# Segmented attention scores over 64 partitions, with a rotary exchange by ScalarE copies

## The chip, the cores and the metric

The program runs on one core of one Trainium2 chip. Its five engines each take instructions in an order fixed when the program is built: TensorE (PE; its weight loads are listed apart as PEld), VectorE (DVE), ScalarE (ACT), GpSimd (POOL) and SyncE (SP), which here issues nearly all DMAs. The metric is the device time of one execution in microseconds; lower is better. Everything on TensorE is fp32 here, and each fp32 product appears in the profile as two matmul instructions with two weight loads.

## The reference

A batch of 16 sequences of 256 tokens with 256 features goes through four residual steps:

```python
x = x + attn0(cross(x, side, embed))             # 16 heads of 16 features, rotary, causal
x = x + ffn0(cond(x, W[cat]))                    # fp4 quantize/dequantize, gate, up, down (704)
x = x + attn1(diffuse(x, zX, zY, zR))            # segmented attention: the change is here
x = x + moe(cond2(x, experts[idx]))              # 8 experts, top 2, one shared
```

The third step, cut to what matters:

```python
q, k, v = split(rmsnorm(seq) * g_norm @ W_qkv)           # 16 heads of 64 features
q = q * cos + rotate_half(q) * sin                       # pairs (even, odd) of features
k = k * cos + rotate_half(k) * sin
q, k, v = segments of 128 tokens                         # two segments a sequence
k = concat(pm[0], k); v = concat(pm[1], v)               # 16 persistent keys a head
p = softmax(where(mask, q @ k.T * 64**-0.5, -1e30))      # 128 x (16 + 128) a head and segment
out = (p @ v) @ W_out
```

## The kernel before

The program has two parts. The first, `woven` (line 292), holds the first three steps. Each is written as one or more generators that yield single operations; `weave` (line 182) is a planner that runs when the program is built. It keeps an estimated time at which each engine is free and each tile is written or read, takes from all generators the operation that can start soonest, and appends it to its engine's queue. Between operations with the same start the generator that stands earlier in the list wins. Costs come from `Unit.cost` (line 165): for a matmul the columns, divided by a factor `side` for small tiles (2 where at most 32 rows are used); for the others a fixed part and a part per element; a DMA costs SP 0.06 us and lands 4.5 us later. In `ready` an operation that overwrites a tile waits for the last write and read of what was there.

The generators in their order: `stage_a` and `stage_e` (first attention), three generators that quantize weights of the feed-forward, `stage_f` (feed-forward; when it ends, batch b may be diffused), `stage_p` (diffusion and projections), `stage_g` (scores and softmax), `stage_v` (values and output projection; at the fourth group of heads it stores x to a DRAM tile `xd`). `g.done` counts what is finished; with it `stage_p` may be three groups of four heads ahead of the values, `stage_g` two, and `stage_a` five batches ahead of the last store. There are 16 batches with four groups, 64 groups in all.

For each group, `project4` (line 897) loads weights (256 KB in two DMAs for q and k, then v and output weights), and computes q and k transposed: features on partitions. Feature pairs are split: tile half r = 0 holds the even features, r = 1 the odd ones, each with four heads of 32 features on 128 partitions. The rotary step is therefore a product with cos and one with sin over both halves (VectorE, tiles `f_t1` and `f_t2`), and a subtraction and an addition between halves (GpSimd, 256 elements each), into `f_q` for q and into `keys[n]` for k. `scores4` (line 955) computes the scores in two passes of two heads. A score of 64 features is two matmuls of 32 partitions, one for each half, added up in PSUM, with the two heads on different 32-partition strips of the array. VectorE then adds the mask and takes the maximum, ScalarE computes the exponentials with their sums, GpSimd multiplies by the reciprocal. `values4` transposes the probabilities and multiplies by the values and the output weights.

`stage_p` begins with what is loaded once: `lap`, cos and sin and their scaled copies, the product of persistent values with the output weights (`pmo`), and the persistent keys, copied into `keys[n]` by 16 GpSimd copies of 32x64.

`project_heads` (line 467) does the first attention's rotary step along the free axis, with a tile for each of the two products. `fetch_a` (line 413) loads a batch's `xT`, `fT`, `emb`, `f` and `x`.

The second part, `mixture` (line 1034), is ordered by the framework's own scheduler. It loads all 16 batches of x from `xd` into `xs`, then `b1`, `bs2`, the shared expert's weights `w1s` and `w2s`, then the weights of `conditioned` (line 1338), which projects 512 tokens at a time with a per-batch weight `own` loaded three deep, and routes the tokens; then shared blocks, expert tiles and combination follow.

Of the kernel before, what the change touches and what calls it, by code (L numbers as in the profile page):

```python
# [12 lines left out]
F32 = mybir.dt.float32  # L13
# [6 lines left out]
P = 128  # L20
# [42 lines left out]
def setup(ctx, tc, a, n_batch):  # L63
# [28 lines left out]
    k.zero = c.tile([P, D], F32, name="zero")  # L92
    nc.gpsimd.memset(k.zero, 0.0)

    k.xd = [dram.tile([S, D], F32, name=f"xd{b}") for b in range(n_batch)]
# [50 lines left out]
class Unit:  # L146
# [17 lines left out]
    def cost(self, fn, outs, ins):  # L164
        if self.name == "SP":
            return 0.06
        if self.name == "PE":
            if fn == "transpose":
                return 0.15
            lhsT, rhs = ins  # L170
            fp32 = 4 if rhs.dtype == F32 else 1
            rows, cols, n = lhsT.shape[0], row_size(lhsT), row_size(rhs)
            side = (2 if rows <= 32 else 1) * (3 if cols <= 32 else 2 if cols <= 64 else 1)
            return max((2 if fp32 == 4 else 1) * cols / 2070, fp32 * n / 2070 / side) + 0.01
        fixed, each = COSTS[self.name]
        n = max(row_size(x) for x in outs[:1] + ins)
        if fn == "reciprocal":
            each = 0.006
        return fixed + each * n + (0.3 if len(outs) > 1 else 0)


def weave(streams):
# [8 lines left out]
    def ready(op, engine):  # L191
# [4 lines left out]
        for x in op.outs:  # L196
# [7 lines left out]
            for p in before:  # L204
                if p:
                    t = max(t, p[0] + (HOP if p[1] != engine else 0.0))
# [85 lines left out]
def woven(k):  # L292
    nc, tc = k.nc, k.tc
    with ExitStack() as ctx:
# [12 lines left out]
        g.live, g.kT = {}, {}  # L307
        g.x, g.io, g.done = {}, {}, {"W": 0, "A": 0, "M": 0, "E": 0, "F": 0, "P": 0, "G": 0, "V": 0, "L": 0}
        with tc.manual_schedule():
            weave([stage_a(g), stage_e(g), stage_gate(g), stage_up(g), stage_down(g), stage_f(g), stage_p(g), stage_g(g), stage_v(g)])  # L310

# [101 lines left out]
def fetch_a(g, b):  # L413

    a = g.a
    g.x[b] = g.xp.tile([P, 2, D], F32, name="x", tag="x")
    xT = g.a_.tile([P, 2, S], F32, name="xT", tag="xT", bufs=2)
    fT = g.a_.tile([P, 2, S], F32, name="fT", tag="fT")
# [48 lines left out]
def project_heads(g, hT):  # L467
# [8 lines left out]
    for st in range(2):  # L476
# [11 lines left out]
        table = lambda t: t[:, st, :].unsqueeze(1).to_broadcast([P, 2 * H, DH0 // 2])  # L488
        t1, t2 = tile_a(g, 2 * D, "b_t1"), tile_a(g, 2 * D, "b_t2")
        for r in range(2):  # L490
            yield g.dve.tensor_tensor(pairs(t1)[:, :, :, r], pairs(qk)[:, :, :, r], table(g.cos0), ALU.mult)
            sin = table(g.sin0 if r else g.nsin0)
            yield g.dve.tensor_tensor(pairs(t2)[:, :, :, r], pairs(qk)[:, :, :, 1 - r], sin, ALU.mult)
        for i, dst in enumerate((qp, kp)):
            half = slice(i * D, (i + 1) * D)
            yield g.pool.tensor_tensor(dst[:, st, :, 0:DH0], by_head(t1[:, half]), by_head(t2[:, half]), ALU.add)

# [298 lines left out]


def stage_p(g):
    k, a = g.k, g.a
    yield lambda: g.done["A"] > 0 and g.done["W"] == 3  # L800
    g.lap, op = load(g, g.w, "lap", [P, 2, S], a["lap"])
# [36 lines left out]

    g.keys = []
    for n in range(4):  # L840
        pmk = tile_l(g, [P, 2, 4 * PM], "pmk", 2)
        yield g.sp.dma_start(out=pmk, in_=a["pmk"][:, n])
        t = g.w.tile([P, 2, 2, PM + P], F32, name=f"keys{n}")
        for j in range(4):
            rows = row32(j, 32)
            src = pmk[rows, :, j * PM : (j + 1) * PM]
            yield g.pool.tensor_copy(t[rows, :, :, 0:PM], src.unsqueeze(2).to_broadcast([32, 2, 2, PM]))
        g.keys.append(t)
    g.mhalf = g.w.tile([P, 2], F32, name="mhalf")
    yield g.pool.memset(g.mhalf, -0.5)  # L850
# [46 lines left out]
def project4(g, n, zT):  # L897

    a = g.a
    wq = tile_l(g, [P, 2, 2, 2 * P], "wq", 2)  # L900
    for which in range(2):
        cols = slice((8 * which + 2 * n) * P, (8 * which + 2 * n + 2) * P)
        yield g.sp.dma_start(out=wq[:, which], in_=a["w_qk1"][:, :, cols])
    wv, wo = tile_l(g, [P, 2, 4 * DH1], "wv", 2), tile_l(g, [P, 2, D], "wo", 3)
    yield g.sp.dma_start(out=wv, in_=a["w_v1"][:, :, n * 4 * DH1 : (n + 1) * 4 * DH1])
    yield g.sp.dma_start(out=wo, in_=a["w_out1"][:, 2 * n : 2 * n + 2, :])
    q = tile_l(g, [P, 2, S], "f_q", 3)
    by_seg = lambda t: t.rearrange("p (s t) -> p s t", s=2)
    for which in range(2):
        one = yield from single(g, wq, zT)  # L910
        pq = one.rearrange("p (r t) -> p r t", r=2)
        for r in range(2):
            yield from mm_(g, pq[:, r, :], [(wq[:, which, c, r * P : (r + 1) * P], zT[:, c, :]) for c in range(2)])
        t1, t2 = tile_l(g, [P, 2, S], "f_t1"), tile_l(g, [P, 2, S], "f_t2")
        cos, sin = (g.cos1, g.sin1) if which else (g.cosq, g.sinq)
        yield g.dve.tensor_tensor(t1, pq, cos.unsqueeze(1).to_broadcast([P, 2, S]), ALU.mult)
        yield g.dve.tensor_tensor(t2, pq, sin.unsqueeze(1).to_broadcast([P, 2, S]), ALU.mult)
        g.singles.append(one)
        dst = [g.keys[n][:, r, :, PM:] if which else by_seg(q[:, r, :]) for r in range(2)]
        yield g.pool.tensor_tensor(dst[0], by_seg(t1[:, 0, :]), by_seg(t2[:, 1, :]), ALU.subtract)  # L920
        yield g.pool.tensor_tensor(dst[1], by_seg(t1[:, 1, :]), by_seg(t2[:, 0, :]), ALU.add)
    v = tile_l(g, [P, 2, 4 * DH1], "f_v", 3)
# [4 lines left out]
    yield copy_(g, v, pv)  # L927
    g.singles.append(one)
    return q, v, wo

# [24 lines left out]
def scores4(g, n, q, v, wo):  # L955
# [8 lines left out]
    for j0 in (0, 2):  # L964
        two = yield from pair(g, q, keys)
        sc = [two[:, i, : 2 * (PM + P)].rearrange("p (s w) -> p s w", s=2) for i in range(2)]
        for st in range(2):
            for r in range(2):
                for i in range(2):
                    rows = row32(j0 + i, 32)  # L970
                    lhsT, rhs = q[rows, r, st * P : (st + 1) * P], keys[rows, r, st, :]
                    yield g.pe.matmul(sc[i][:, st, :], lhsT, rhs, start=r == 0, stop=r == 1)
        for i in range(2):
# [60 lines left out]
def mixture(k, out):  # L1034
# [5 lines left out]
    with ExitStack() as ctx:  # L1040
# [33 lines left out]
        for blk in range(early, NT // 4):  # L1074
# [5 lines left out]
            for t in range(4 * blk, 4 * blk + 4):  # L1080
                combine(k, r, t, out)


# [254 lines left out]
def conditioned(k, keep, r):  # L1338
# [3 lines left out]
    with ExitStack() as ctx:  # L1342
# [178 lines left out]
```

## Time and profile before

| What | Value |
|---|---|
| Median of 3 runs (lowest, highest) | 2903.49 us (2898.98, 2906.39) |
| Profiled execution | 2904.1 us |
| Its span | 2902.4 us |
| Mean granted TensorE clock | 0.964 |
| End of the woven part (last operation on x) | 1896.8 us |
| First conditioned matmul after it | 1926.8 us |
| DMA moved | 270.38 MB |

The span is the time from the first to the last recorded instruction. A group of instructions is listed by line, engine, operation and tiles (written <- read), its shape, its count, its busy time and mean in ns, and the idle time of its engine just before it with what ended that. Line 160 is the planner's helper, through which all operations of the woven part pass, so there the tiles tell which code an operation belongs to. [...]

The page's slices show the same in rough form: 40 equal slices of 72.6 us, a digit for tenths of busy time. The shared and expert blocks take the slices at the end.

```profile
PE 5899999999999999999999998869999999999999
DVE  6566666676676667766776665613332000000023
ACT  2223323333333333333333333313222222222221
POOL 4333333333334334433343333312331000000034
PEclk8799999999899999998999999979999999999999
```

### The profile page before, as it was taken

The page shows a single profiled execution, that of the slowest core. Times are in us where ns is not written, and L with a number is a line of the kernel's source. Part 1 is how long each engine was busy: PE and PEld are TensorE (multiplying, and loading weights), DVE is VectorE, ACT ScalarE, POOL GpSimd, SP SyncE. Part 2 cuts the span into 40 slices and gives each one's busy share as a digit, 9 for nine tenths or more (in the row PEclk, how much of TensorE's full clock was granted, in tenths as well). Part 3 has the DMA queues.
Part 4 walks back from the last instruction along what each step waited for, and adds up shares of the span by engine and source line. Part 5 has one row for each costly group of instructions (what it writes and reads, how often), then busy time and mean ns, then how long its engine had stood idle before and what let it go on. Part 6 is the DMA issues. An engine that isn't in the chain of part 4 may idle for free. (4 is left out here: it accounts for less than half of the span.)

```text
span 2902.4 us, 41871 instructions
## 1 busy us (share of the span) xinstructions
PE 2728.9 (94%) x15819; PEld 2056.7 (71%) x15819; DVE 1437.1 (50%) x3115; ACT 925.0 (32%) x2416; POOL 862.8 (30%) x1030
## 2 busy tenths in 40 slices
PE   5899999999999999999999998869999999999999
PEld 3666667777777777777677767735566788888866
DVE  6566666676676667766776665613332000000023
ACT  2223323333333333333333333313222222222221
POOL 4333333333334334433343333312331000000034
PEclk8799999999899999998999999979999999999999
DMA  3132122222131231231231122141112255555533
GB/s 109 55 95 74 53 90 70 65 93 70 59 99 59 67 101 45 74 108 35 79 104 44 62 88 66 52 144 46 49 48 84 76 190 191 191 193 201 192 100 106
DMA packets 196525, 270.38 MB, mean 93 GB/s; under 512 B 34912, under 2 KB 167264, under 8 KB 186976
## 3 DMA queue, kind: packets, MB, share of 16 engines
q1 hardware_dynamic: 190176, 250.87, 26.9%
q0 software_dynamic: 6144, 16.79, 1.9%
q8 instruction: 127, 2.08, 0.3%
q14 instruction: 78, 0.64, 0.1%
HBM read 207.05 MB, written 60.56 MB: 92 GB/s over the span
## 5 line engine op out<-in xcount | busy, mean ns | idle before, releaser
L160 ACT ACTIVATE f_prob<-pair,f_stat 128x144 f32<-128x144 f32 x512 | 191.1, 378 | 270.1 <-DVE f_stat L160 258.6
L160 DVE TENSOR_TENSOR pair<-pair,mask 128x256 f32<-128x256 f32 (+1 forms) x384 | 197.8, 515 | 123.1 <-PE pair L160 83.2
L160 PE MATMUL single<-e_zT,wq 128*128 128x256 f32 x1024 | 254.0, 392 | 0.0
L49 PE MATMUL bank<-ysT,w 128*128 128x256 f32 x1120 | 247.5, 379 | 0.2 <-ACT ysT L113 0.2
L1162 POOL DMA_INDIRECT got<-osort,pos_o x64 | 62.4, 974 | 623.5 <-PE bank L49 582.5
L49 PE MATMUL bank<-w,ehT 128*128 128x256 f32 x1120 | 247.5, 379 | 0.0
L1144 ACT ACTIVATE ehT<-bank,own_b 128x256 f32<-128x256 f32 x280 | 132.8, 474 | 348.8 <-PE bank L49 348.8
L49 PEld LDWEIGHTS bank<-ysT,w 128*128 128x128 f32 x1120 | 212.7, 190 | 29.4 <-ACT ysT L113 0.5
L49 PEld LDWEIGHTS bank<-w,ehT 128*128 128x128 f32 x1120 | 210.2, 190 | 27.2
L160 PEld LDWEIGHTS single<-e_zT,wq 128*128 128x128 f32 x1024 | 193.4, 196 | 32.8 <-issue 2.8
L160 POOL TENSOR_SCALAR_AFFINE_SELECT b_e<-b_e 128x512 f32<-128x512 f32 x128 | 86.8, 678 | 329.5 <-ACT b_e L160 329.5
L160 PE MATMUL pair<-keys,f_q 32*128 32x144 f32 x2048 | 164.9, 300 | 0.9 <-ACT b_e L160 0.7
L160 PEld LDWEIGHTS pair<-keys,f_q 32*128 32x128 f32 x2048 | 137.2, 190 | 35.9 <-issue 28.0
L160 ACT ACTIVATE b_e<-pair 128x768 f32<-128x768 f32 x128 | 103.7, 811 | 166.2 <-PE pair L160 153.5
L1152 DVE TENSOR_TENSOR eo<-bank,eb 128x512 f32<-128x512 f32 x35 | 24.2, 692 | 234.4 <-PE bank L49 234.4
L160 POOL TENSOR_TENSOR f_q<-f_t,f_t 128x256 f32<-128x256 f32 x128 | 91.8, 736 | 160.7 <-DVE f_t L160 151.3
L160 PE MATMUL single<-wo,f_oT 128*128 128x256 f32 x512 | 129.8, 386 | 9.5 <-ACT f_oT L160 8.4
L160 PE MATMUL pair<-b_qkT 16*128 16x128 f32 (+1 forms) x1024 | 126.9, 371 | 10.9 <-ACT b_qkT L160 7.9
L160 DVE TENSOR_REDUCE qpad<-pair 128x2 f32<-128x256 f32 (+1 forms) x256 | 131.0, 554 | 4.4
L160 DVE TENSOR_TENSOR x<-x,single 128x512 f32<-128x512 f32 (+1 forms) x112 | 68.0, 607 | 128.5 <-PE single L160 127.9
L160 POOL TENSOR_TENSOR keys<-f_t,f_t 128x256 f32<-128x256 f32 x128 | 95.3, 764 | 118.6 <-DVE f_t L160 117.5
L160 PE MATMUL pair<-b_qS,b_qkT 17*128 17x256 f32 (+1 forms) x1024 | 121.7, 357 | 6.2 <-DVE qpad L160 2.8
(290 smaller groups left out, 5235.7 us busy)
## 6 DMA issues: line engine op xcount, KB each, us to landing
w<-in_w SPq DMA_DIRECT2D x70, 1024.0 KB
ysort<-zero SPq DMA_DIRECT2D x32, 1024.0 KB
wq<-in_w_qk SPq DMA_DIRECT2D x128, 256.0 KB
wv<-in_w_v SPq DMA_DIRECT2D x64, 256.0 KB
wo<-in_w_out SPq DMA_DIRECT2D x64, 256.0 KB
ys<-ysort SPq DMA_DIRECT2D x35, 256.0 KB
osort<-eo SPq DMA_DIRECT2D x35, 256.0 KB
eb<-in_b SPq DMA_DIRECT2D x35, 128.0 KB
```

The source lines that it names most:

```text
L49: nc.tensor.matmul(out, lhsT, rhs, start=start and i == 0, stop=stop and i == last)
L160: return Op([(self.name, self.cost(fn, outs, aps), lambda: call(*args, **kw))], outs, aps)
L1144: nc.scalar.activation(hT[:, f, :], ph, AF.Gelu_apprx_tanh, bias=b1[:, f : f + 1])
L1152: nc.vector.tensor_tensor(o, po, b2.unsqueeze(1).to_broadcast([P, 2, D]), ALU.add)
L1162: nc.gpsimd.indirect_dma_start(out=g, out_offset=None, in_=k.osort[:, :], in_offset=bass.IndirectOffsetOnAxis(ap=r.pos_o[:, i, t : t + 1], ...
```

## The change

It has several parts.

- **Scores over 64 partitions.** A head's 64 features now lie together: even ones on 32 partitions, odd ones on the next 32. Two heads fill 128 partitions, and c counts two pairs of heads. A score is one matmul of 64 partitions, so `scores4` issues half as many.
- **Rotary exchange.** The partner of a feature is now on another strip of 32 partitions. After the sin product, ScalarE copies `t2` strip by strip into `t3` with neighbouring strips exchanged, four copies of 32 partitions by 512 elements for q and four for k; the sign is put into the sin tables once. GpSimd then adds once over 512 elements. That addition is yielded one step later (`join`). `f_t1` gets two buffers, `f_t3` has two, `f_t2` one.
- **Weights in the new order.** `stage_order` loads the q and k weights in eight steps, re-orders the columns with two GpSimd copies a step, and stores them to a DRAM tile `wqk`, from which `project4` then loads. The list of generators holds it twice, and each runs all eight steps. `stage_p` waits until the first has ended.
- **Persistent keys.** Eight small loads and four wider copies in place of four loads and sixteen copies.
- **Order.** `stage_g` stands before `stage_p`. The planner prices 33 to 64 rows with factor 1.5, and no longer holds an SP operation back for an earlier write or read by SP.
- **First attention.** The cosine product is done in place in `qk`, after the sine products; `xT` has one buffer.
- **Mixture.** Only batches 0 and 1 of x are loaded at the start, the others two ahead in `conditioned`; `w1s` and `w2s` are loaded after it.

```diff
@@ class Unit: cost; weave: ready
-            side = (2 if rows <= 32 else 1) * (3 if cols <= 32 else 2 if cols <= 64 else 1)
+            side = (2 if rows <= 32 else 1.5 if rows <= 64 else 1) * (3 if cols <= 32 else 2 if cols <= 64 else 1)
...
-                if p:
+                if p and not p[1] == engine == "SP":
                     t = max(t, p[0] + (HOP if p[1] != engine else 0.0))
@@ woven
-            weave([stage_a(g), stage_e(g), stage_gate(g), stage_up(g), stage_down(g), stage_f(g), stage_p(g), stage_g(g), stage_v(g)])
+            weave([stage_a(g), stage_e(g), stage_gate(g), stage_up(g), stage_down(g), stage_order(g), stage_order(g), stage_f(g), stage_g(g), stage_p(g), stage_v(g)])
@@ fetch_a
-    xT = g.a_.tile([P, 2, S], F32, name="xT", tag="xT", bufs=2)
+    xT = g.a_.tile([P, 2, S], F32, name="xT", tag="xT")
@@ project_heads
-        t1, t2 = tile_a(g, 2 * D, "b_t1"), tile_a(g, 2 * D, "b_t2")
+        t2 = tile_a(g, 2 * D, "b_t2")
         for r in range(2):
-            yield g.dve.tensor_tensor(pairs(t1)[:, :, :, r], pairs(qk)[:, :, :, r], table(g.cos0), ALU.mult)
             sin = table(g.sin0 if r else g.nsin0)
             yield g.dve.tensor_tensor(pairs(t2)[:, :, :, r], pairs(qk)[:, :, :, 1 - r], sin, ALU.mult)
+        for r in range(2):
+            yield g.dve.tensor_tensor(pairs(qk)[:, :, :, r], pairs(qk)[:, :, :, r], table(g.cos0), ALU.mult)
...
+def stage_order(g):
+
+    k = g.k
+    for i in range(8):
+        cols = slice(i * 2 * P, (i + 1) * 2 * P)
+        raw, out = tile_l(g, [P, 2, S], "f_t1", 2), tile_l(g, [P, 2, S], "f_t3", 2)
+        yield g.sp.dma_start(out=raw, in_=g.a["w_qk1"][:, :, cols])
+        for c in range(2):
+            dst = out[:, c].rearrange("p (j r d) -> p j r d", j=4, r=2)
+            yield g.pool.tensor_copy(dst, raw[:, c].rearrange("p (r j d) -> p j r d", r=2, j=4))
+        yield g.sp.dma_start(out=k.wqk[:, :, cols], in_=out)
+    g.done["O"] = 1
@@ stage_p
-    yield lambda: g.done["A"] > 0 and g.done["W"] == 3
+    yield lambda: g.done["A"] > 0 and g.done["W"] == 3 and g.done["O"]
...
+    for rows in (row32(1, 32), row32(3, 32)):
+        for t in (g.sin1, g.sinq):
+            yield g.pool.tensor_scalar(t[rows], t[rows], -1.0, None, ALU.mult)
@@ project4
-        yield g.sp.dma_start(out=wq[:, which], in_=a["w_qk1"][:, :, cols])
+        yield g.sp.dma_start(out=wq[:, which], in_=k.wqk[:, :, cols])
...
-        t1, t2 = tile_l(g, [P, 2, S], "f_t1"), tile_l(g, [P, 2, S], "f_t2")
+        t1, t2, t3 = (tile_l(g, [P, 2, S], f"f_t{i}", 1 if i == 2 else 2) for i in (1, 2, 3))
...
-        dst = [g.keys[n][:, r, :, PM:] if which else by_seg(q[:, r, :]) for r in range(2)]
-        yield g.pool.tensor_tensor(dst[0], by_seg(t1[:, 0, :]), by_seg(t2[:, 1, :]), ALU.subtract)
-        yield g.pool.tensor_tensor(dst[1], by_seg(t1[:, 1, :]), by_seg(t2[:, 0, :]), ALU.add)
+        for i in range(4):
+            yield g.act.copy(t3[row32(i, 32)], t2[row32(i ^ 1, 32)])
+        dst = g.keys[n][:, :, :, PM:] if which else q.rearrange("p c (s t) -> p c s t", s=2)
+        yield from join
+        join = iter([g.pool.tensor_tensor(dst, by_seg(t1), by_seg(t3), ALU.add)])
@@ scores4
-            for r in range(2):
-                for i in range(2):
-                    rows = row32(j0 + i, 32)
-                    lhsT, rhs = q[rows, r, st * P : (st + 1) * P], keys[rows, r, st, :]
-                    yield g.pe.matmul(sc[i][:, st, :], lhsT, rhs, start=r == 0, stop=r == 1)
+            for i in range(2):
+                rows, c = row32(2 * i, 64), j0 // 2
+                lhsT, rhs = q[rows, c, st * P : (st + 1) * P], keys[rows, c, st, :]
+                yield g.pe.matmul(sc[i][:, st, :], lhsT, rhs, start=True, stop=True)
@@ mixture, conditioned
-        for b in range(B):
-            nc.sync.dma_start(out=k.xs[:, 2 * b : 2 * b + 2, :], in_=k.xd[b].rearrange("(s p) d -> p s d", p=P))
+        for b in range(2):
+            load_x(k, b)
...
+        conditioned(k, keep, r)
         nc.sync.dma_start(out=w1s, in_=a["w1"][NE])
         nc.sync.dma_start(out=w2s, in_=a["w2"][NE])
-        conditioned(k, keep, r)
...
+                if b + 2 < B:
+                    load_x(k, b + 2)
```

More of the change, by code (lines that the diff above doesn't have):

```diff
@@ L93, in setup @@
     nc.gpsimd.memset(k.zero, 0.0)
+    k.wqk = dram.tile([P, 2, 2 * H * DH1], F32, name="wqk")
     k.xd = [dram.tile([S, D], F32, name=f"xd{b}") for b in range(n_batch)]
@@ L307, in woven @@
         g.live, g.kT = {}, {}
-        g.x, g.io, g.done = {}, {}, {"W": 0, "A": 0, "M": 0, "E": 0, "F": 0, "P": 0, "G": 0, "V": 0, "L": 0}
+        g.x, g.io, g.done = {}, {}, {"W": 0, "O": 0, "A": 0, "M": 0, "E": 0, "F": 0, "P": 0, "G": 0, "V": 0, "L": 0}
         with tc.manual_schedule():
-            weave([stage_a(g), stage_e(g), stage_gate(g), stage_up(g), stage_down(g), stage_f(g), stage_p(g), stage_g(g), stage_v(g)])
+            weave([stage_a(g), stage_e(g), stage_gate(g), stage_up(g), stage_down(g), stage_order(g), stage_order(g), stage_f(g), stage_g(g), stage_p(g), stage_v(g)])
 def load(g, pool, name, shape, src):
@@ L488, in project_heads @@
         table = lambda t: t[:, st, :].unsqueeze(1).to_broadcast([P, 2 * H, DH0 // 2])
-        t1, t2 = tile_a(g, 2 * D, "b_t1"), tile_a(g, 2 * D, "b_t2")
+        t2 = tile_a(g, 2 * D, "b_t2")
         for r in range(2):
-            yield g.dve.tensor_tensor(pairs(t1)[:, :, :, r], pairs(qk)[:, :, :, r], table(g.cos0), ALU.mult)
             sin = table(g.sin0 if r else g.nsin0)
             yield g.dve.tensor_tensor(pairs(t2)[:, :, :, r], pairs(qk)[:, :, :, 1 - r], sin, ALU.mult)
+        for r in range(2):
+            yield g.dve.tensor_tensor(pairs(qk)[:, :, :, r], pairs(qk)[:, :, :, r], table(g.cos0), ALU.mult)
         for i, dst in enumerate((qp, kp)):
             half = slice(i * D, (i + 1) * D)
-            yield g.pool.tensor_tensor(dst[:, st, :, 0:DH0], by_head(t1[:, half]), by_head(t2[:, half]), ALU.add)
+            yield g.pool.tensor_tensor(dst[:, st, :, 0:DH0], by_head(qk[:, half]), by_head(t2[:, half]), ALU.add)
 def row32(j, n):
@@ L839, in stage_p @@
     g.keys = []
+    pmk = tile_l(g, [P, 4, 2, PM], "pmk")
+    for j in range(4):
+        for r in range(2):
+            src = a["pmk"][row32(j, 32), :, r, j * PM : (j + 1) * PM]
+            yield g.sp.dma_start(out=pmk[row32(2 * (j % 2) + r, 32), :, j // 2, :], in_=src)
     for n in range(4):
-        pmk = tile_l(g, [P, 2, 4 * PM], "pmk", 2)
-        yield g.sp.dma_start(out=pmk, in_=a["pmk"][:, n])
         t = g.w.tile([P, 2, 2, PM + P], F32, name=f"keys{n}")
[L844 to L847, printed above, removed]
+        yield g.pool.tensor_copy(t[:, :, :, 0:PM], pmk[:, n].unsqueeze(2).to_broadcast([P, 2, 2, PM]))
         g.keys.append(t)
+    for rows in (row32(1, 32), row32(3, 32)):
+        for t in (g.sin1, g.sinq):
+            yield g.pool.tensor_scalar(t[rows], t[rows], -1.0, None, ALU.mult)
     g.mhalf = g.w.tile([P, 2], F32, name="mhalf")
@@ L897, in project4 @@
 def project4(g, n, zT):
-    a = g.a
+    k, a = g.k, g.a
     wq = tile_l(g, [P, 2, 2, 2 * P], "wq", 2)
@@ L907, in project4 @@
     q = tile_l(g, [P, 2, S], "f_q", 3)
-    by_seg = lambda t: t.rearrange("p (s t) -> p s t", s=2)
+    by_seg = lambda t: t.rearrange("p c (s t) -> p c s t", s=2)
+    join = ()
     for which in range(2):
@@ L928, in project4 @@
     g.singles.append(one)
+    yield from join
     return q, v, wo
@@ L1081, in mixture, with load_x @@
                 combine(k, r, t, out)
+def load_x(k, b):
+    k.nc.sync.dma_start(out=k.xs[:, 2 * b : 2 * b + 2, :], in_=k.xd[b].rearrange("(s p) d -> p s d", p=P))
 def shared_block(k, r, w1, w2, blk):
```

## The prediction

> **What bounds the kernel now.** I read the page first (busy shares, slices, chain), then the stretches by stage, then the groups by shape, then the order of time around the scores and around the hand-over to the mixture. The chain that ended last holds only the final shared block, so it says nothing on the place of the change.
>
> ```profile
> span 2902.4 us, 41871 instructions
> PE 2728.9 (94%) x15819; PEld 2056.7 (71%) x15819; DVE 1437.1 (50%) x3115; ACT 925.0 (32%) x2416; POOL 862.8 (30%) x1030
> ```
>
> TensorE is busy for 94% of the span, the next engine for half. An average over stages proves little, so next come the stretches: the woven stage with all streams, its tail (mostly segmented attention), the hand-over, the conditioned projection, and the start in two parts. Columns are start and end, length, busy time of PE, PEld, DVE, ACT and POOL, clock, DMA share, GB/s.
>
> ```profile
> 300.00:1700.00 1400.00, 1338.49 (x9191) 1011.11 (x9192) 959.91 (x1922) 508.57 (x1499) 533.66 (x635) 0.97 0.23 72
> 1700.00:1896.80 196.80, 172.89 (x1162) 139.44 (x1161) 108.08 (x213) 65.24 (x246) 67.30 (x81) 0.92 0.21 69
> 1896.80:1926.80 30.00, 4.20 (x18) 3.28 (x18) 1.83 (x8) 0.62 (x2) 3.47 (x15) 0.54 1.00 310
> 1926.80:2280.00 353.20, 350.46 (x1239) 212.21 (x1239) 104.53 (x402) 98.09 (x144) 79.98 (x72) 1.00 0.16 50
> ...
> 0.00:20.00 20.00, 0.22 (x1) 0.22 (x2) 1.23 (x3) 1.28 (x1) 6.78 (x16) 1.00 0.57 185
> 20.00:100.00 80.00, 65.23 (x331) 44.05 (x332) 55.14 (x117) 25.44 (x57) 34.74 (x44) 0.74 0.27 79
> ```
>
> From 300 to 1700 us TensorE idles 61.5 us of 1400 (4%); VectorE is at 69%, ScalarE at 36%. So TensorE sets the pace, and work taken from it there comes off the end, unless another engine starts to make it wait. In the tail it idles 24 of 197 us. In the hand-over it idles 26 of 30 us while the DMA engines are full (share 1.00, 310 GB/s). The groups that the change touches or copies:
>
> ```profile
> L160 PE MATMUL pair<-keys,f_q 32*128 32x144 f32 x2048 | 164.9, 300 | 0.9 <-ACT b_e L160 0.7 <-DVE vpad L160 0.2
> L160 POOL TENSOR_TENSOR keys<-f_t,f_t 128x256 f32<-128x256 f32 x128 | 95.3, 764 | 118.6 <-DVE f_t L160 117.5
> L160 POOL TENSOR_TENSOR f_q<-f_t,f_t 128x256 f32<-128x256 f32 x128 | 91.8, 736 | 160.7 <-DVE f_t L160 151.3 <-PE single L160 4.7 <-DVE f_stat L160 4.0
> L160 ACT COPY f_pT<-single 128x512 f32<-128x512 f32 x94 | 53.3, 587 | 55.5 <-PE single L160 53.3 <-DVE q_y L160 1.9
> ```
>
> Each fp32 product is recorded as two instructions: the code asks for 1024 score products, the profile shows 2048. In order of time, one pair of heads is 16 instructions:
>
> ```profile
> 1022.41 1.25 PE L160 MATMUL pair<-keys,f_q 32*128 32x144 f32 x16
> 1023.59 1.99 PE L160 MATMUL single<-wv,e_zT 128*128 128x256 f32 x8
> 1025.52 0.86 PE L160 MATMUL single<-b_e,vpad 128*32 128x256 f32 x16
> 1026.30 1.09 PE L160 MATMUL single<-f_pT,f_v 128*64 128x128 f32 x16
> 1027.33 0.44 PE L160 MATMUL single<-ident,b_oS 128*128 128x128 f32 x2
> ```
>
> From the start of the scores to the start of the next group: 1.18 us. The values (f_pT, f_v) are 16 instructions of 128 columns, two at a time: 1.03 us. Recorded ends overlap the next start, so starts are what to subtract.
>
> **What the Trainium skill says.** "TensorEngine Tiling (Array Packing)", section Tiling Modes: 64 rows by 128 columns is two tiles that run independently, 32 by 128 is four. "TensorE: Matmul & The Clock Gate", section Why this matters for your kernels: one matmul over 32 rows takes as long as one over 128; the gain is in running tiles at once. The trace agrees: eight full 128-row instructions of 256 columns (e_zT,wq at 1035.68, the next group at 1037.41) take 1.73 us, 0.85 ns a column, and sixteen score instructions of 144 columns at that rate would take 1.95 us one after another; they take 1.18, so they run two at a time. "ScalarE: Activation LUTs", section What ACT_TABLE_LOAD costs: an ACTIVATE with immediate operands takes 186 ns plus 0.833 ns an element, back-to-back ones overlapping by about 93 ns; for 512 elements 613 ns, the trace has 587. That ScalarE's queue is strictly first in, first out ("TensorE: Matmul & The Clock Gate", the table at its head) is what makes the added copies a risk.
>
> **Part by part.**
>
> Scores. Before, two heads run at once, each in two steps of 32 features; after, two heads at once, each in one step of 64. Of 16 instructions in a group 8 are left. Two at a time, a group takes half of 1.95, 0.97 us, plus 0.21 us of changing over to make 1.18; after, 0.48 + 0.21 = 0.69. The 0.2 is confirmed by the values: 16 x 128 x 0.85/2 ns = 0.87, measured 1.03. So 0.49 us less for each of 64 x 2 = 128 groups, 63 us at full clock. The page's mean group (164.9/128 = 1.29 against 1.25 us undisturbed) is 3% longer for the clock: 64 us. Bounds: the kernel's planner now prices 64 rows at 1.5 instead of 2 tiles' worth; if that is true, a group takes 0.64 + 0.21 = 0.85 and 42 us go; nothing supports more than 75 us (1.18/2 each).
>
> Rotary exchange. ScalarE gets 64 x 2 x 4 = 512 copies of 32 partitions by 512 elements. No row has 32 partitions from SBUF; the nearest is 587 ns (f_pT, from PSUM), the skill's price less overlap is 520. I take 587: 300 us more, 925 to 1225 us. In 300 to 1700 (46 of the 64 head groups) it is 46 x 4.7 = 216 us, so ScalarE goes from 36% to about 53%. GpSimd: 256 additions of 256 elements (187 us) become 128 of 512; at 1.28 us (a_qT's 1289 ns) 164 us, 23 us less. VectorE is unchanged. None of this is on TensorE. The path from projection to q or keys grows by 4 x 0.587 - 3 x 0.09 = 2.1 us and two hand-overs. Projections may be three head groups ahead of the values, about 3 x 27 us in the middle, so the latency is covered; without cover it would be 2.5 us x 64 = 160 us. What is not covered is the queue: behind four copies stand exponentials and PSUM evacuations that TensorE waits for (f_oT, f_pT, b_qkT: 17 of the 61.5 us idle), and on GpSimd, behind an addition waiting for its copies, stand b_e's masks and the quantization (d_h, c_y: 24 of the 61.5 us). The bounds are 0 (all planned around) and 100 us (one full block of copies, 2.1 us, at three out of four head groups). ScalarE's load grows by half, so I let the ScalarE and GpSimd part of the waits (50 us) grow by 30%: +15 us, tail included.
>
> Order. Scores get rank over projections. TensorE work is the same; in the tail it may shorten or lengthen the 24 us idle. I take 0 and leave +-10 in the range.
>
> The re-ordered weights. Two streams of eight steps each run the whole re-ordering twice: 16 loads and 16 stores of 256 KB, 8.4 MB, and 32 GpSimd copies of 128x256 (about 0.86 us, the cost of cosq's scaling of that shape: 27 us). At 310 GB/s the bytes are 27 us of DMA time; the first 100 us carry 100 GB/s, so they fit, but loads of weights queue behind them, and SP's queue stands while a store waits for its copy. Their SP instructions, 32 at about 0.45 us, are 14 us of a queue that waits most of the time. GpSimd goes from 42 to about 69 us in the first 100, and it carries the weight quantization, which gates the first feed-forward at about 101 us. TensorE idles 20 us at first anyhow. Bounds 0 and 40 us; I take +8.
>
> Hand-over. 14 of 16 loads of xs (8.7 of 9.9 us of SP's issue) and w1s and w2s (1.5 us) leave the front of SP's queue, with 3.7 + 2.1 = 5.8 MB. expb, issued at 1917.9 and the one that the first conditioned matmuls waited for (till 1924.6), is issued 10.2 us sooner, and 5.8 MB less at 310 GB/s is 18.7 us less queue. I take -12, bounds -5 and -19. The later loads come behind exp_w, a block (44 us) ahead of use, in a stage at 50 GB/s: hidden, and if not, 256 KB at 310 GB/s, 0.8 us each. w1s and w2s are needed about 2280 us, some 40 us after their new place.
>
> Edits with one answer: in-place cosine product (same four VectorE instructions; GpSimd still reads before the next is written), xT with one buffer (fT, loaded next, has one already), fewer but wider pm copies (4.3 us become about 5 with the sign changes, once), the planner's rule for SP after SP: 0, with SP's queue possibly standing some us at a time.
>
> **Sum**, against the profiled execution (2904.1 us, span 2902.4; the median of the runs is 2903.5, so no correction): -64 + 15 + 8 - 12 = -53, 2851 us.
>
> **Rivals.**
> A, as above: 2851, its own range 2815 to 2880. For it: 96% TensorE in the stage.
> B, 64-row tiles pack worse (1.5): -42 + 15 + 8 - 12 = -31, 2873. For it only the planner's constant; against it the values' rate.
> C, slower: ScalarE's queue takes the pace. Each of the 64 head groups adds two blocks of 2.1 us in front of exponentials; if 1.7 us of the 4.2 end up as TensorE idle, 64 x 1.7 = 109 us, and 2904 - 64 + 109 + 8 - 12 = 2945; with 1.2 us 2913. It decides from about 1.1 us a head group, where it has eaten 68 us. For it: exponentials already make GpSimd and VectorE wait, and in the tail a head group takes 12 us, of which copies would take 4.7 of ScalarE. Against it: ScalarE is half empty, and the planner prices copies about right.
> D, the start: the doubled re-ordering delays the first feed-forward by its full 40 us: 2883. For it, SP and GpSimd both in order; against it, its streams rank below those that load the weights.
>
> **How the numbers follow.** A 0.53, B 0.11, C 0.25 (2910 to 2960), D 0.11. A difference under 0.3% (9 us, 2895 to 2912) can't be told from none. Faster: A, B and D, with a tail of D and A taken off, 0.68; within: 0.08; slower: C, 0.24. The range goes from 2815 to 2925, which takes in A, B, D and the lower half of C. A alone has 2815 to 2880.
>
> **What would show it.** Scores as 64x144 x1024 with about 85 to 90 us busy and 0.69 us from start to start (B: 0.85). ScalarE 300 us more. TensorE idle in the woven stage up by no more than 25 us, waits for ScalarE or GpSimd grown by 15 (C: 80 and more). First conditioned matmul 10 to 15 us after the last store of x. First projection e_zT,wq at 187 us before, under 200 after (D: 220 and more). I am wrong if the stage's idle time grows by as much as its busy time shrinks.

## The result, and the profile after

The changed kernel takes 2981.57 us (median of four runs, 2972.64 to 2988.36), the kernel before beside it 2904.94 us: a ratio of 1.0264, 95% interval 1.0231 to 1.0297. It is 77 us slower; the forecast was 53 us faster. The profiled execution took 2988.4 us, 84 us more than that of before.

The page of the changed kernel: its first lines, then four engines and the granted clock in 40 slices of 74.7 us.

```profile
span 2986.6 us, 40424 instructions
PE 2735.1 (92%) x14795; PEld 2030.8 (68%) x14795; DVE 1478.6 (50%) x3157; ACT 1221.1 (41%) x2886; POOL 852.3 (29%) x926
PE   5899999979989999999889997769999999999999
DVE  6456667565777766676667775533343000000013
ACT  2234455445545455444545465533232232222221
POOL 5323233333433423333333332322332000000035
PEclk7779999899999999999999998879999999999999
```

TensorE has 1024 instructions fewer, and yet it is busy 6 us longer (2735.1 against 2728.9). Before, 9s ran almost unbroken through the woven part; now 7s and 8s stand in slices 9 and 12, in the middle (20 and 21) and in three slices at its end (25 to 27).

The stretches of the changed kernel (start and end, length, busy time of PE, PEld, DVE, ACT and POOL, clock, DMA share, GB/s): the same 1400 us as before, the rest of the woven part, the hand-over, the conditioned projection, and last the woven part from its first projection (`e_zT,wq`) to its end. Below it the same last stretch of the kernel before.

```profile
300.00:1700.00 1400.00, 1288.17 (x8120) 948.38 (x8122) 957.06 (x1888) 702.48 (x1767) 491.24 (x518) 0.95 0.21 68
1700.00:1996.80 296.80, 240.43 (x1370) 185.28 (x1368) 161.05 (x310) 160.11 (x443) 96.86 (x88) 0.91 0.21 68
1996.80:2011.00 14.20, 2.22 (x11) 1.87 (x11) 1.10 (x6) 0.64 (x2) 1.13 (x14) 0.56 0.80 224
2011.00:2360.00 349.00, 345.85 (x1225) 208.58 (x1225) 105.94 (x401) 98.17 (x144) 81.27 (x73) 1.00 0.22 68
205.80:1996.80 1791.00, 1614.46 (x10001) 1195.32 (x9999) 1182.24 (x2329) 905.73 (x2305) 622.97 (x643) 0.94 0.21 68
```

```profile
187.10:1896.90 1709.80, 1616.02 (x11025) 1226.51 (x11024) 1145.13 (x2289) 610.09 (x1833) 646.52 (x771) 0.97 0.23 71
```

The account of the 84 us closes with these. The first projection comes 18.7 us later (205.8 against 187.1). From there to the end of the woven part it takes 1791.0 us in place of 1709.8, 81.2 more. The hand-over is 15.7 us shorter (14.2 against 29.9). After it nothing differs. So the loss lies in the woven part, and there TensorE's idle time went from 93.8 us to 176.5, while its busy time stayed (1616.0, 1614.5) although a thousand instructions left it.

Why did it stay? The groups that the change touches, and one that it doesn't, by shape, after:

```profile
L161 PE MATMUL pair<-keys,f_q 64*128 64x144 f32 x1024 | 104.1, 318 | 9.9 <-POOL keys L161 9.0 <-ACT b_e L161 0.5 <-ACT f_prob L161 0.3
L161 PE MATMUL single<-e_zT,wq 128*128 128x256 f32 x1024 | 274.2, 415 | 41.2 <-DMA wq<-wqk 38.8 <-ACT e_zT L161 2.4
L161 ACT COPY f_t<-f_t 32x512 f32<-32x512 f32 x512 | 316.0, 617 | 146.4 <-DVE f_t L161 137.9 <-POOL f_q L161 0.6 <-DVE f_stat L161 0.4
L161 POOL TENSOR_TENSOR keys<-f_t,f_t 128x512 f32<-128x512 f32 x64 | 83.9, 1311 | 64.5 <-ACT f_t L161 63.6
```

The second of them before:

```profile
L160 PE MATMUL single<-e_zT,wq 128*128 128x256 f32 x1024 | 254.0, 392 | 0.0
```

The scores gave up 60.8 us (164.9 to 104.1). But 1024 instructions that nobody touched now take 415 ns each in place of 392, while the mean granted clock of the stretch fell from 0.97 to 0.94. (The granted clock is the share of its full clock that TensorE was given. The median instruction of this group takes 379 ns, the longest 792; in the trace the granted clock of a moment is either 1 or 0.5.) Summed over the stretch, the untouched instructions took back 59 us (-1.6 + 60.8). And a new wait stands in front of this group: 38.8 us for the DMA of `wq`, of which before had none. The lists of waits suggest where it comes from. Two of TensorE's and two of SP's longest waits after:

```profile
PE single L161 <- POOL f_prob L161: 39.1, 17, 6.4
PE single L161 <- DMA wq<-wqk: 38.8, 9, 6.1
...
SPq L161 <- PE single L161: 1011.2, 93, 57.1
SPq L161 <- DVE x L161: 345.8, 13, 53.7
```

Columns are total, times and longest, in us. SP waits 346 us for VectorE's last write of x, that is, at the store of x; before it did so for 67.1 us.

All of TensorE's waits in this stretch, summed by what they were for, account for nearly all of its idle time: GpSimd 56.1 us before and 71.2 after, ScalarE 25.0 and 27.8, VectorE 10.5 and 36.2, DMA 0 and 38.8. So of the 83 us more, only 18 are waits that ended with ScalarE or GpSimd; the rest ended with loads of weights and with VectorE.

One wait for weights in order of time, SP's issues and the TensorE group that suffers:

```profile
648.12 0.39 SPq L161 DMA_DIRECT2D xd<-x  x1
648.61 0.42 SPq L161 DMA_DIRECT2D xT<-in_xT  x1
649.08 0.44 SPq L161 DMA_DIRECT2D fT<-in_fT  x1
...
651.76 1.18 SPq L161 DMA_DIRECT2D wq<-wqk  x2
...
657.61 3.43 PE L161 MATMUL single<-e_zT,wq 128*128 128x256 f32 x8 [6.14 <-DMA wq<-wqk]
```

Once the store is let go at 648.12, the next batch's inputs are issued, and only then the weights. TensorE stands 6.14 us for them, and the group that follows is recorded with 3.43 us where the same eight instructions take 1.89 elsewhere. This gap so costs twice: itself, and the slower clock behind it. Of the 15 stops of TensorE over 3 us in the stretch, 14 are followed by a clock of 0.5.

### The profile page after: what moved, and what is told of

Its sections match the earlier page's. It is cut to its first block, busy times and chain, and to the rows that moved or that the text cites. A ratio compares the mean times of both kernels' runs of the same rounds, so it can differ in the third digit from the quotient of the medians.

```text
span 2986.6 us, 40424 instructions
## 1 busy us (share of the span) xinstructions
PE 2735.1 (92%) x14795; PEld 2030.8 (68%) x14795; DVE 1478.6 (50%) x3157; ACT 1221.1 (41%) x2886; POOL 852.3 (29%) x926
## 5 line engine op out<-in xcount | busy, mean ns | idle before, releaser
L161 ACT COPY f_t<-f_t 32x512 f32<-32x512 f32 x512 | 316.0, 617 | 146.4 <-DVE f_t L161 137.9
L161 PE MATMUL single<-e_zT,wq 128*128 128x256 f32 x1024 | 274.2, 415 | 41.2 <-DMA wq<-wqk 38.8
L161 PEld LDWEIGHTS single<-e_zT,wq 128*128 128x128 f32 x1024 | 203.2, 207 | 83.1 <-issue 33.6
L161 PE MATMUL pair<-b_qkT 16*128 16x128 f32 (+1 forms) x1024 | 134.5, 385 | 17.2 <-DVE qpad L161 5.6
L161 PE MATMUL single<-wo,f_oT 128*128 128x256 f32 x512 | 135.8, 400 | 9.0 <-ACT f_oT L161 6.0
L161 PE MATMUL single<-wv,e_zT 128*128 128x256 f32 x512 | 131.5, 402 | 0.0
L161 PEld LDWEIGHTS pair<-b_qS,b_qkT 17*128 17x128 f32 x1024 | 99.2, 203 | 45.9 <-issue 10.6
L161 POOL TENSOR_TENSOR f_prob<-f_prob,f_stat 128x1024 f32<-128x1024 f32 x64 | 124.1, 1939 | 0.0
```

The lines of the kernel that those rows point to most:

```text
L161: return Op([(self.name, self.cost(fn, outs, aps), lambda: call(*args, **kw))], outs, aps)
```

## The experiments

Sixteen kernels ran. The median of before beside them lay between 2901.7 and 2904.1 us. "Tail" is the stretch after the last feed-forward matmul, with nine to twelve groups of heads left, by the count of score matmuls: its length, and TensorE's idle time in it. "wq" is TensorE's wait for the DMA of q and k weights over the whole run. "Rank" is the place of `stage_g` and `stage_p` in the list of generators. Ratios are to before.

| Run | Median, us | Ratio [95%] | Tail, idle | wq |
|---|---|---|---|---|
| before | 2904.9 | 1 | 167, 21 | none |
| after | 2981.6 | 1.0264 [1.0231, 1.0297] | 206, 48 | 38.8 |
| e1: SP rule undone | 2941.5 | 1.0141 [1.0097, 1.0184] | 216, 56 | 12.5 |
| e2: rank undone | 2916.9 | 1.0054 [1.0039, 1.0070] | 158, 28 | 1.1 |
| e3: no re-ordering on the chip | 2961.8 | 1.0216 [1.0175, 1.0257] | 206, 48 | 38.5 |
| e4: no copies | 2809.2 | 0.9685 [0.9659, 0.9712] | 134, 15 | none |
| e5: rank, SP rule, re-ordering undone | 2857.7 | 0.9844 [0.9828, 0.9861] | 170, 34 | 0.2 |
| e6: copies that nothing reads | 2977.7 | 1.0263 [1.0246, 1.0280] | 201, 48 | 31.3 |
| e7: no copies, rank and SP rule undone | 2863.6 | 0.9871 [0.9850, 0.9891] | 134, 15 | none |
| e8: before with the mixture's part | 2889.0 | 0.9953 [0.9936, 0.9969] | 167, 21 | none |
| e9: after, another plan | 3009.1 | 1.0367 [1.0350, 1.0384] | 210, 50 | 29.9 |
| e10: e5, another plan | 2889.1 | 0.9956 [0.9940, 0.9973] | 173, 33 | 1.1 |
| e11: no copies, SP rule undone | 2858.3 | 0.9855 [0.9837, 0.9874] | 134, 15 | none |
| e12: no copies, rank undone | 2870.9 | 0.9891 [0.9875, 0.9908] | 152, 16 | none |
| e13: after, a third plan | 2963.7 | 1.0213 [1.0182, 1.0245] | 196, 45 | 14.4 |
| e14: e5, a third plan | 2876.3 | 0.9911 [0.9881, 0.9941] | 149, 31 | 0.4 |
| e15: before, another plan | 2917.4 | 1.0046 [1.0032, 1.0061] | 158, 15 | none |
| e16: before with scores ahead | 2895.1 | 0.9971 [0.9960, 0.9983] | 172, 23 | 1.5 |

**One part undone at a time.** First the three parts that touch no arithmetic.

e1, the planner's old rule for SP:

```diff
-                if p and not p[1] == engine == "SP":
+                if p:
```

> The changed kernel with one part undone: the planner again holds an SP operation back for an earlier write or read by SP. Queue theory (the loads of a batch, 1.1 MB, are now queued straight behind the store of x and in front of the q and k weights, and the 38.8 us for which TensorE waits for wq plus the slower clock after each such gap are most of the 77 us): 2920 to 2935 us, and the waits for wq fall under 10 us. Copy theory (ScalarE's copies lengthen every wait) and rank theory (projections come too late because they stand behind the scores): 2970 to 2985 us, no more than the spread of the runs.

e2, projections ahead of scores again:

```diff
-stage_g(g), stage_p(g), stage_v(g)])
+stage_p(g), stage_g(g), stage_v(g)])
```

> The changed kernel with stage_p before stage_g again. Rank theory: projections run up to three groups ahead again, their weights are asked for earlier and the keys are ready, so the waits for wq, f_prob and keys (38.8, 39.1 and 9.0 us) fall by half or more: 2890 to 2925 us. Queue theory: the loads stay late, 2965 to 2985. Copy theory: 2970 to 2985.

e3, the weights come with their columns in the new order (the transposition that lays out the input is changed), so that nothing is re-ordered on the chip:

```diff
-stage_order(g), stage_order(g), stage_f(g)
+stage_f(g)
...
-    yield lambda: g.done["A"] > 0 and g.done["W"] == 3 and g.done["O"]
+    yield lambda: g.done["A"] > 0 and g.done["W"] == 3
...
-in_=k.wqk[:, :, cols])
+in_=a["w_qk1"][:, :, cols])
```

> The changed kernel without stage_order: the arrays are handed over with the columns of q and k already in the new order, as they were handed over in the old order before; no loads, copies and stores at the start. Start theory: the first projection comes at 187 us as before and not at 206, so 2960 us (19 us less) and not less than 2950. If the loads from the DRAM tile wqk were slow in themselves, the waits for wq would go too, and it would be 2930.

Each gives something back: 65 us the rank, 40 the SP rule, 20 the re-ordering. e2 and e3 lie in the ranges of the rank theory and the start theory; e1 lies between its two ranges. In e2 the wait for `wq` is all but gone and the tail is 49 us shorter (with ten groups left in place of eleven or twelve); in e1 the wait falls from 38.8 to 12.5 us and the tail stays. In e3 the first projection is back at 191.2 us, 15 us sooner, and little else has changed.

**The three together.** e5 has all three edits, and computes all that the changed kernel does.

> The changed kernel with three parts undone at once: stage_p before stage_g, the planner's rule for SP, and no stage_order (columns handed over in the new order). If the three costs found alone (65, 40 and 20 us) are separate, 2855 to 2870 us, faster than before. If rank and SP rule are two views of one wait (projections that ask for their weights late), about 2890 to 2900 us: 65 and 20 only.

2857.7 us: the three gains add up (65 + 40 + 20 = 125, measured 124), and this version is faster than both kernels. So the loss lies with the order of the work and of the weights, and not in the new way to compute the scores taken by itself. (That the sum fits to 1 us is luck: two more plans of e5, below, lie 19 and 31 us higher.) The remaining parts of the change (the price of 1.5, the addition one step later, the single buffer of `xT`, the cosine product in place) were not undone one by one; e5 holds them all and is fast.

**The copies.** e4 leaves the 512 copies out; the addition takes the sin product as it is, so that q and k get the wrong partner's product. The sin product also gets the two buffers that the copies' target had.

```diff
-        for i in range(4):
-            yield g.act.copy(t3[row32(i, 32)], t2[row32(i ^ 1, 32)])
...
-by_seg(t1), by_seg(t3), ALU.add
+by_seg(t1), by_seg(t2), ALU.add
```

> The changed kernel with the exchange left out: the 512 ScalarE copies are gone and GpSimd adds the cosine and the unexchanged sine products, so q and k are not rotated. Copy theory: 300 us less on ScalarE and 2.5 us less on each path give 50 to 75 us back, 2905 to 2930 us. Queue and rank theories: ScalarE was at half load and had room, so 2960 to 2980 us.

e6 makes the copies, and the addition doesn't read them (the same part of the computation is changed as in e4). The sin product gets the two buffers, the copies' target one:

```diff
-by_seg(t1), by_seg(t3), ALU.add
+by_seg(t1), by_seg(t2), ALU.add
```

> The changed kernel with all 512 ScalarE copies made, but GpSimd adds the unexchanged product (q and k are not rotated), so nothing waits for the copies but the next use of their tile. Occupation theory (what costs is 316 us in ScalarE's queue in front of exponentials and evacuations): near the changed kernel, 2940 to 2980 us. Path theory (what costs is that q and keys come 2.5 us later, after a hand-over more): near the kernel without the exchange, 2809 to 2840 us.

e4 is 172 us faster than the changed kernel, far below both of its ranges; e6 is only 4 us faster, in the range of the occupation theory. So it isn't the way through the copies that costs, from projection to q or keys, but that ScalarE is occupied by them; nor is it the wait for a free buffer, for VectorE's products never wait for the copies in e6's list of waits. That seems to put all the blame on the copies, but e5 has them too. e7 is e4 with the old rank and SP rule:

> The kernel without the exchange (2809 us), with stage_p before stage_g and the planner's old rule for SP. If order and rule cost in themselves, 2720 to 2750 us. If they cost only where the exchange makes the projections late, 2800 to 2815 us.

e7 lies outside of both ranges. Here the copies' absence is worth next to nothing: 2863.6 without, 2857.7 with them (e5, which also lacks the re-ordering, some 20 us by e3). By these runs the copies cost much under the new order only, and the new order costs only with the copies.

**Is it real, or the luck of a plan?** `weave` takes the operation that can start soonest, so any touch changes the whole sequence. e9 and e10 alter one constant of the planner that has nothing to do with the change, in the changed kernel and in e5:

```diff
-TURN = 0.1
+TURN = 0.12
```

> The changed kernel whole, with one number of the planner altered that no part of the change touches: what it charges TensorE for turning to another generator, 0.12 us in place of 0.10. It asks how much the planner's order, and with it the time, moves for no reason of its own. If the costs of rank and of SP's rule are real effects of where these put the operations, this run stays within 20 us of the changed kernel (2962 to 3002 us). If they are scatter of a greedy plan, of the size that any touch of the planner brings, it lies 40 us or more away on either side.

> The same alteration (0.12 in place of 0.10) in the version with rank, SP's rule and the weights' order undone, which took 2857.7 us. Real effects: 2840 to 2876 us. Scatter: as far as 2900 us and more. If it and the changed kernel with the same alteration both keep their places, the 124 us between them are the order's.

Both fell outside of the bounds given for real effects, and short of those for scatter, having moved by 28 and 31 us in the same direction; the distance between them stayed at 120. A constant that the change doesn't touch is here worth 30 us. e13 and e14 have 0.08 in its place, e15 is the kernel before with 0.12:

> The changed kernel whole, the planner's charge for turning to another generator at 0.08 us in place of 0.10; a third plan of the same program. The two so far took 2981.6 and 3009.1 us. If the new order costs time in itself, this one is above 2940 us too, and its stage after the last feed-forward again idles TensorE 45 us or more. If the two were unlucky plans, it lies below 2920 us.

> The version with rank, SP's rule and the weights' order undone, with 0.08 us in place of 0.10; a third plan of it. The two so far took 2857.7 and 2889.1 us. If it is really faster than the kernel before, this one is below 2900 us, with 28 to 36 us of idle TensorE after the last feed-forward. If the two were lucky plans, it is above 2910 us.

> The kernel before whole, 0.12 us in place of 0.10. It measures how much of the difference to the kernel before is the accident of that kernel's own plan. If its plan is a lucky one, this run takes 30 us more or worse (2930 and up); if it is ordinary, 2880 to 2925 us.

Three plans of the changed kernel: 2963.7, 2981.6, 3009.1. Three of e5: 2857.7, 2876.3, 2889.1. The means, 2984.8 and 2874.4, are 110 us apart, and the closest two plans 75. Two of before: 2904.9 and 2917.4. So the effect of the three parts together is real, and all three plans of e5 are faster than both of before; its slowest, e10, by little (0.9956, interval 0.9940 to 0.9973), no more than the mixture's part brings by itself (e8, below). But single differences of 20 to 40 us, as e1 and e3 show, can't be told from a different plan. Nor can what stands beside them in the trace: another plan of the changed kernel (e13) waits for `wq` only 14.4 us, about as little as e1, and the first projection comes at 202.8 and 230.5 us in the changed kernel's other two plans, at 181.9 and 213.6 in e5's.

**Which part of the order meets the copies?** e11 and e12 are e4 with one part undone each, and e16 puts scores ahead in the kernel before.

> Without the exchange's 512 copies (q and k not rotated), scores ahead of projections, but SP's old rule: the version without copies took 2809.2 us, and the one with both old rank and old rule 2863.6. It tells which of the two is what helps where ScalarE is free. If it is SP's rule (loads sooner), this run stands at 2850 to 2865; if it is the rank, at 2805 to 2820.

> Without the exchange's 512 copies (q and k not rotated), SP's new rule, but projections ahead of scores again. If the rank is what cost time only with a loaded ScalarE, this run stands at 2850 to 2865 us (the old rank worse without copies, as both together were); if the rank by itself does nothing here and SP's rule does, at 2805 to 2820.

```diff
-stage_p(g), stage_g(g), stage_v(g)])
+stage_g(g), stage_p(g), stage_v(g)])
```

> The kernel before with scores put ahead of projections and nothing else, so without the exchange's copies on ScalarE. If scores ahead cost time by themselves, it takes 2950 us or more. If they cost only where ScalarE carries the copies, it stays within the scatter of a plan, 2870 to 2935 us.

By its expectation e11 would give the gain of e4 to SP's rule, while e12 fits neither of its ranges. Together they say something else: without copies, three of four plans lie at 2858 to 2871 whichever rank and rule they have, and e4's 2809 is the odd one. No second plan of e4 was run, so whether that is a lucky plan or a gain of rank and rule together is open. 42 of the 52 us that e4's stretch from the first projection to the end of the woven part is shorter than e11's are the clock: the same matmuls, busy for a shorter time (e4, then e11):

```profile
202.30:1819.30 1617.00, 1536.27 (x10001) 1139.48 (x9999) 1161.13 (x2264) 616.84 (x1858) 629.25 (x643) 0.99 0.24 75
196.80:1865.50 1668.70, 1577.92 (x10000) 1170.30 (x10000) 1148.11 (x2289) 597.88 (x1831) 628.88 (x641) 0.96 0.23 73
```

e16 answers the question of the rank: scores ahead cost nothing in the kernel before (2895.1 against 2904.9). With the copies the same step costs 65 us, more than the 45 between the changed kernel's own three plans. All pairs side by side, medians in us (other plans of the same version in brackets):

| Order | With copies | Without copies | Cost of the copies |
|---|---|---|---|
| scores ahead, SP's new rule | 2981.6, after (2963.7, 3009.1) | 2809.2, e4 | 172 |
| scores ahead, SP's old rule | 2941.5, e1 | 2858.3, e11 | 83 |
| projections ahead, SP's new rule | 2916.9, e2 | 2870.9, e12 | 46 |
| projections ahead, SP's old rule | 2857.7, e5, no re-ordering on the chip (2876.3, 2889.1) | 2863.6, e7, with it | not alike |

A single entry can be off by some 30 us, but the groups don't overlap: all six kernels with copies and scores ahead (e3 and e6 too) took 2941 us or more, all four with copies and projections ahead 2857 to 2917, all four without copies 2871 or less.

The tail shows the same meeting in one stage, and its idle time hardly scatters. The stretch after the last feed-forward matmul (columns as above), first in the changed kernel:

```profile
1790.50:1996.80 206.30, 157.89 (x878) 121.99 (x874) 100.28 (x201) 106.66 (x305) 58.69 (x53) 0.87 0.20 62
```

In e5, with the copies but projections ahead:

```profile
1700.20:1870.10 169.90, 135.99 (x814) 106.17 (x812) 92.53 (x185) 98.53 (x282) 53.37 (x49) 0.92 0.19 60
```

In e11, with scores ahead but no copies:

```profile
1731.80:1865.50 133.70, 118.91 (x774) 94.36 (x770) 86.32 (x171) 48.05 (x190) 49.30 (x46) 0.99 0.22 69
```

ScalarE (the fourth busy time) doubles with the copies, to half of the stretch and more. TensorE idles 48, 34 and 15 us, at clocks of 0.87, 0.92 and 0.99. In all runs: copies and scores ahead 45 to 56 us, copies and projections ahead 28 to 34, no copies 15 and 16 (the kernel before and its variants: 15 to 23). What TensorE waits for in the tail of the changed kernel, and on GpSimd what the additions wait for:

```profile
PE single L161 <- POOL f_prob L161: 25.3, 9, 6.4
PE single L161 <- DMA wq<-wqk: 6.5, 2, 4.2
PE pair L161 <- POOL keys L161: 3.8, 2, 1.9
...
POOL keys L161 <- ACT f_t L161: 40.4, 8, 7.2
```

The normalised probabilities come late, and so do the loads of weights and the keys. e5 waits for `f_prob` nearly as long (23.8 us), and its additions into the keys wait for the copies nearly as long too (33.7 us). So of the 14 us between the two the waits for weights and keys are the larger named part (10.3 us against 1.0).

SP's wait at the store of x sorts the runs too: 276 to 455 us in all six with copies and scores ahead (after, e1, e3, e6, e9, e13), 33 to 151 with copies and projections ahead, 9 to 31 without copies, 196 in e16. Where it is long together with the copies, TensorE waits for weights (12.5 to 38.8 us). That SP's standing causes the rest of the idle time isn't shown: e1 has 416 us of it and waits for `wq` only 12.5. Which instruction carries the rank's effect from ScalarE's queue to TensorE was not isolated either.

**The mixture alone.** e8 is the kernel before with the edits of `mixture` and `conditioned`:

> The kernel before with the mixture part of the change alone: two batches of x at the start, the others two ahead in the conditioned stage, w1s and w2s after it. The hand-over fell from 29.9 to 14.2 us in the changed kernel, so 2885 to 2889 us; 2902 if what is saved there comes back as a wait in the conditioned or shared blocks.

13.6 us faster by the medians (2888.95 against 2902.54), and the hand-over takes 13.4 us in place of 29.9. This part is a gain by itself, and no accident of a plan: the woven part is the kernel before's. What the same place looks like in the changed kernel (the last write of x, and two groups of TensorE after it):

```profile
1996.10 0.69 DVE L161 TENSOR_TENSOR x<-x,single 128x512 f32<-128x512 f32 x1 [4.54 <-PE single L161]
2008.78 0.36 PE L49 MATMUL bank<-onehot,expb 16*64 16x16 f32 x2 [12.79 <-DMA expb<-in_L_cond_experts_b]
...
2010.98 2.60 PE L49 MATMUL bank<-g_xT,fc 128*128 128x512 f32 x4
```

It is still the load of `expb` that ends the wait, only sooner, with most loads of x and those of `w1s` and `w2s` no longer issued before it.

## Why the prediction was wrong

**Scores: right.** Eight instructions to a pair of heads, 0.69 us from start to start, as worked out; in the changed kernel, in order of time:

```profile
1021.70 0.76 PE L161 MATMUL pair<-keys,f_q 64*128 64x144 f32 x8
1022.39 0.92 PE L161 MATMUL pair<-b_qS,b_qkT 17*128 17x256 f32 x8
```

Busy time fell by 60.8 us for the 64 foretold (B would have had 0.85 and 42); the 85 to 90 us named as a sign were too low, it is 104.1, as recorded ends overlap the next start. But "work taken from it there comes off the end, unless another engine starts to make it wait" had its second half come true.

**Order: the step that failed.** "TensorE work is the same ... I take 0 and leave +-10 in the range." Scores ahead cost 65 us in the changed kernel (e2), and nothing in the kernel before (e16). The prediction priced rank and copies apart and added the prices; in the runs each costs most where the other is there. In the sum two things stood at nothing: waits of TensorE for anything but ScalarE and GpSimd ("VectorE is unchanged"; the loads of weights were not priced as a wait), and a slower clock. The first grew by 64.5 us (38.8 for loads of weights, 25.7 for VectorE), the second came to 59 us of busy time. With the rank undone (e2) the waits for weights and VectorE are at 1.1 and 18.7 us, and those for ScalarE at 51.8 in place of 27.8. How the copies on ScalarE make weights and VectorE late is open, as said above. That the copies would be "all planned around" relied on the plan of before, which the change replaced.

**Exchange: its own waits right, its cost too small.** "+15 us, tail included" was meant for TensorE's waits for ScalarE and GpSimd, and these grew by 18 us (81.1 to 99.0). But the whole cost of the copies is 46 us with projections ahead (e2 against e12; under SP's old rule it can't be told from scatter), and with scores ahead 83 us (e1 against e11) to 172 (after against e4), up to and beyond the 100 that was given as the bound. The tail alone idles 12 to 19 us more even in the good order, which uses up the whole 15. ScalarE's added 296 us (925.0 to 1221.1; 300 foretold) is right.

**SP's rule: "0, with SP's queue possibly standing some us at a time".** It stands 346 us at the store of x, up to 53.7 at a time; but with the old rule it is 416 (e1) and with the old rank 53 (e2), so the standing goes with the rank. In time the rule is 40 us in one plan, not told from scatter, and so is the fall of TensorE's waits for weights from 38.8 to 12.5 us.

**Re-ordered weights: +8 taken, 18.7 measured** to the first projection, inside the bounds of 0 to 40. The copies were cheaper than thought (32 of 0.455 us, for 0.86). Undoing the re-ordering (e3) or the SP rule (e1) brings back 15 us each, to 191 us. Other plans move this start by more (181.9 to 230.5 us, see above), so the 18.7 can't be put down to the re-ordering alone; one of them (e13) would have passed for D.

**Hand-over: -12 taken, -15.7 measured** by the stretch, -13.6 by time alone (e8). Right.

**Rivals.** C, ScalarE's queue takes the pace, had the sign and the resource: e6 shows that ScalarE's occupation and not the latency costs. But its own mark, 80 us and more of waits for ScalarE or GpSimd, didn't come (18). It had "1.1 us a head group" as the point from which it decides; the 83 to 172 us are 1.3 to 2.7 us for each of 64. But C was drawn as a property of the copies, at 2910 to 2960 us, without the order that brings it about. The mark set for error, idle time growing as much as busy time shrinks, came true with more: 83 us more idle, and the busy time kept up by the slower clock. That e5 took 2857.7, near the forecast of 2851, is partly luck: the sum without the re-ordering is -61 us, and its three plans lie 47, 29 and 16 us below before.

## What to carry to other kernels

Costs of parts needn't add: price a new load on a second engine together with the new order of the queues, and look hardest at the stage with least to hide it (here the tail, where 21 us of idle time became 48). Where a greedy planner writes the order, measure its scatter first by moving a constant that should not matter; here that moved the time by up to 31 us, and a part worth less can't be judged from one plan. Try the parts of a large change apart: three edits with no arithmetic in them turned a gain of 1.6% (e5) into a loss of 2.6%.

## What the hardware showed that was not expected

Long idle gaps on TensorE slow what follows, but they are not the only thing that does. "TensorE: Matmul & The Clock Gate", section Why this matters for your kernels, warns of idle gaps above about 3 us between bursts of matmuls. The trace agrees where gaps are long: after the gap of 6.14 us the group took 3.27 us to the next one's start (657.61 to 660.88), against 1.73 for the same eight instructions undisturbed. Yet in the changed kernel's stretch from the first projection to the end of the woven part, about half of the 225 us at a clock of 0.5 lie neither in a stop over 2 us nor in the 7 us after one, and e11, with a single stop over 2 us in that stretch, has 130 us at 0.5, where e4 has 31. The same matmuls are busy 1614 us there (after, mean clock 0.94), 1578 (e11, 0.96) and 1536 (e4, 0.99), with 176, 91 and 81 us idle. What sets the clock between e11 and e4 was not found. That the long gaps alone made the changed kernel's clock slow is therefore not shown.

ScalarE's copies of 32 partitions didn't overlap: four of 512 elements take 2.50 us together (at 1919.50 in the changed kernel), 617 ns each. The estimate of 613 ns from what "ScalarE: Activation LUTs", section What ACT_TABLE_LOAD costs, gives for one with immediate operands fits, the overlap of about 93 ns that it gives for back-to-back ones doesn't show for these copies. For exponentials something like it does: one of 0.38 us at 1916.20 is followed by the engine's next instruction after 0.27.
